# Chebyshev and attention node maps: four blocks of nodes per product, weights on the diagonal, and the product taken term by term

## The chip, the cores and the metric

The kernel runs on one core of one Trainium2 chip. The metric is the time of one execution on the device in microseconds (us). The core has engines that work side by side: TensorE (PE) multiplies and transposes, VectorE (DVE) and ScalarE (ACT) work on elements, GpSimd (POOL) here mostly issues gathers, and SyncE (SP) issues transfers. SP, ACT and POOL each have a queue of their own for transfers, and each engine carries out its instructions in order.

## The reference

A graph network of four layers works on 12500 nodes with 32 features (`x`) and 200000 edges (`src`, `dst`, sorted by `dst`). After each layer the result is added to `x` and normalised. The layer that matters here is the second, two Chebyshev convolutions and one attention. Its `reference` calls come down to this:

```python
def unnL(f):                      # sum of the neighbours' rows
    return segment_sum((f * dinv)[src], dst, n) * dinv
for layer in range(2):            # the same weights W (96 x 32) and b both times
    X0 = feat
    X1 = -re_norm * unnL(X0) + X0 * (re_norm - 1)
    X2 = -2 * re_norm * unnL(X1) + X1 * 2 * (re_norm - 1) - X0
    feat = leaky_relu(concatenate([X0, X1, X2], 1) @ W + b, 0.01)
fs = feat @ Ws + bs               # attention: both maps are 32 x 32
fd = feat @ Wd + bd
e = leaky_relu(fs[src] + fd[dst], 0.2)
# logits e . attn, softmax over the edges of each dst, weighted sum of fs[src]
```

The other three layers are two tensor products over the edges and a plain segment sum.

## The kernel before, in words

The 12500 nodes lie in 98 blocks (`NB`) of 128, one node in each partition, so that a node array is a tile of 128 x 98 x 32. Before the second layer a step of its own scatters the number of edges between pairs of nodes into a matrix of eight-bit counts in memory. A segment sum, `sums` (L657 to L738), then has two halves that run side by side. For the nodes with many edges it multiplies this matrix, loaded piece by piece (L687 alternately on the queues of SP and ACT, L695 on SP), with the rows of the table on PE (L691, L696). For the other nodes POOL gathers the rows of the edges one group of 128 at a time (L715), DVE builds a comparison matrix (L729), and PE and DVE add the rows to their nodes. Before any of this, `sums` loads the indices of the edges (`src`, L669, on SP) and clears the accumulator (L675, DVE).

In front of each sum stands the making of the table. DVE scales X (L788), `split3` (L486 to L489, alternately ACT and DVE) splits it into three 16-bit parts, and `store_table` writes the two halves of the table to memory on the queues of SP (L519) and ACT (L520). The first gather needs the table and the indices.

A Chebyshev layer is: copy X0 (L783, ACT); twice a table and a sum (called c00, c01 in the first layer, c10, c11 in the second) and the elementwise tail (L793 to L798, DVE and ACT); then the dense product with the 96 x 32 weights `wch`. X0, X1 and X2 lie beside each other in one tile `X` with 96 columns for each block. For each block PE transposes 128 x 96 (L805), ACT copies four transposed blocks at once out of PSUM (L807), PE multiplies each with `wch` (L810: the transposed block is the stationary operand, the 32 columns of the weights move), and DVE adds the bias (L811). The leaky rectifier over all nodes (L813) ends the layer.

The attention map has the same form with one source, `h`: transposes of 128 x 32 (L827), copies (L829), products with both 32 x 32 weights, 64 moving columns (L832), and two additions into `fs` and `fd` (L835). Then `fs` is stored as the attention's table and `fd` is split in three (L486 to L489). The attention begins with the load of the edges' indices (L196, SP) and gathers (L207, POOL); it adds the gathered rows at L894.

The order of the instructions on each engine is that in which the program writes them, except that a scheduler lets an instruction pass ahead where its operands allow it; so the clearing of the attention's accumulator (L843, 128 x 9900) stands ahead of the rectifier L813 on DVE. Buffers come from pools whose places overlap when their lives don't; a tile that takes over a place waits for the last use of the tile before it.

Of the kernel before, what the change touches and what calls it, by code (L numbers as in the profile page):

```python
# [11 lines left out]
F32 = mybir.dt.float32  # L12
# [6 lines left out]
ALU = mybir.AluOpType  # L19
AX = mybir.AxisListType  # L20
PSUM = bass.MemoryType.PSUM
# [4 lines left out]
P = 128  # L26
N, E, D, M = 12500, 200000, 32, 8

NB = -(-N // P)
# [31 lines left out]
class Graph:  # L61
# [4 lines left out]
    def __init__(self, ctx, tc, a):  # L66
# [23 lines left out]
        with tc.tile_pool(name="pre", bufs=1) as pre, \  # L90
# [153 lines left out]
class Counts:  # L244
# [12 lines left out]
    def order(self, row16):  # L257
# [5 lines left out]
        with tc.tile_pool(name="row", bufs=1) as rp, \  # L263
# [216 lines left out]
def split3(nc, pool, name, y, shape, y3=None):  # L480

    *outer, n = shape
    if y3 is None:
        y3 = pool.tile([P, *outer, 3, n], BF16, name=f"{name}3")
    r = pool.tile([P, *outer, n], F32, name=f"{name}r")
    nc.scalar.copy(y3[:, :, 0, :], y)  # L486
    nc.vector.tensor_tensor(r, y, y3[:, :, 0, :], op=ALU.subtract)  # L487
    nc.scalar.copy(y3[:, :, 1, :], r)
    nc.vector.tensor_tensor(y3[:, :, 2, :], r, y3[:, :, 1, :], op=ALU.subtract)  # L489
    return y3  # L490
# [22 lines left out]
def store_table(nc, table, x):  # L513

    if len(x.shape) == 4:
        x = x.rearrange("p b k d -> p b (k d)")
    to = table.rearrange("(b p) d -> p b d", p=P)
    h = NB // 2
    nc.sync.dma_start(to[:, :h, :], x[:, :h, :])  # L519
    nc.scalar.dma_start(to[:, h:, :], x[:, h:, :])  # L520
# [3 lines left out]
def kernel(ctx: ExitStack, tc: tile.TileContext, a: dict, out: bass.AP):  # L524
    nc = tc.nc
    gr = Graph(ctx, tc, a)
    ident = gr.ident
# [11 lines left out]
    x = node.tile([P, NB, D], F32, name="x")  # L539
# [213 lines left out]

    with tc.tile_pool(name="l1", bufs=1) as one, ExitStack() as after:
        h = one.tile([P, NB, D], F32, name="h")
        wch = one.tile([3 * D, D], F32, name="wch")
        nc.sync.dma_start(wch, a["cheb_W"])
        wsd = one.tile([D, 2, D], F32, name="wsd")
        nc.sync.dma_start(wsd[:, 0, :], a["gat_W_src"])
        nc.sync.dma_start(wsd[:, 1, :], a["gat_W_dst"])  # L760
        bch = one.tile([P, D], F32, name="bch")
        nc.sync.dma_start(bch, a["cheb_b"][None, :].to_broadcast([P, D]))
        bsd = one.tile([P, 2, D], F32, name="bsd")
# [10 lines left out]
        nc.vector.tensor_scalar(re[:, 1:2], re[:, 4:5], 2.0, -1.0, op0=ALU.mult, op1=ALU.add)  # L774
        nc.vector.tensor_scalar(re[:, 2:4], re[:, 0:2], 2.0, None, op0=ALU.mult)

        with tc.tile_pool(name="cheb", bufs=1) as cp:
            X = cp.tile([P, NB, 3 * D], F32, name="X")
            t = cp.tile([P, NB, D], F32, name="t")
            y3 = cp.tile([P, NB, 3, D], BF16, name="y3")  # L780
            dinv_b = dinv[:, :, None].to_broadcast([P, NB, D])
            for layer in range(2):
                nc.scalar.copy(X[:, :, 0:D], x if layer == 0 else h)  # L783
                for k in range(2):

                    xk = X[:, :, k * D:(k + 1) * D]
                    xn = X[:, :, (k + 1) * D:(k + 2) * D]
                    nc.vector.tensor_tensor(t, xk, dinv_b, op=ALU.mult)  # L788
                    table = tables3[2 * layer + k]
                    with tc.tile_pool(name=f"sp{layer}{k}", bufs=1) as sp:  # L790
                        store_table(nc, table, split3(nc, sp, "y", t, (NB, D), y3))
                    sums(f"c{layer}{k}", table, y3, t)
                    nc.vector.tensor_tensor(t, t, dinv_b, op=ALU.mult)  # L793
                    nc.scalar.activation(xn, xk, AF.Copy, scale=re[:, 2 * k + 1:2 * k + 2])
                    nc.vector.scalar_tensor_tensor(xn, t, re[:, 2 * k:2 * k + 1], xn, op0=ALU.mult,
                                                   op1=ALU.add)
                    if k == 1:
                        nc.vector.tensor_tensor(xn, xn, X[:, :, 0:D], op=ALU.subtract)  # L798
                with tc.tile_pool(name=f"mm{layer}", bufs=3) as work, \
                        tc.tile_pool(name=f"mmps{layer}", bufs=2, space=PSUM) as psum:  # L800
                    for b in range(0, NB, 4):
                        n = min(4, NB - b)
                        pt = psum.tile([3 * D, 4, P], F32, name="pt")
                        for k in range(n):
                            nc.tensor.transpose(pt[:, k, :], X[:, b + k, :], ident)  # L805
                        xt = work.tile([3 * D, 4, P], F32, name="xt")
                        nc.scalar.copy(xt[:, :n, :], pt[:, :n, :])  # L807
                        po = psum.tile([P, 4, D], F32, name="po")
                        for k in range(n):
                            nc.tensor.matmul(po[:, k, :], xt[:, k, :], wch, start=True, stop=True)  # L810
                        nc.vector.tensor_tensor(h[:, b:b + n, :], po[:, :n, :],  # L811
                                                bch[:, None, :].to_broadcast([P, n, D]), op=ALU.add)
                    nc.vector.scalar_tensor_tensor(h, h, 0.01, h, op0=ALU.mult, op1=ALU.max)  # L813
# [5 lines left out]
        with tc.tile_pool(name="gmm", bufs=3) as work, \  # L819
                tc.tile_pool(name="gmmps", bufs=2, space=PSUM) as psum:  # L820
            fs = work.tile([P, NB, D], F32, name="fs", bufs=1)
            fd = work.tile([P, NB, D], F32, name="fd", bufs=1)
            for b in range(0, NB, 4):
                n = min(4, NB - b)
                pt = psum.tile([D, 4, P], F32, name="pt")
                for k in range(n):
                    nc.tensor.transpose(pt[:, k, :], h[:, b + k, :], ident)  # L827
                xt = work.tile([D, 4, P], F32, name="xt")
                nc.scalar.copy(xt[:, :n, :], pt[:, :n, :])  # L829
                po = psum.tile([P, 4, 2, D], F32, name="po")  # L830
                for k in range(n):
                    nc.tensor.matmul(po[:, k, :, :].rearrange("p a d -> p (a d)"), xt[:, k, :],  # L832
                                     wsd.rearrange("p a d -> p (a d)"), start=True, stop=True)
# [14 lines left out]
        with tc.tile_pool(name="selp", bufs=1) as sp:  # L848
            m = sp.tile([3 * C, C], F32, name="m")
# [135 lines left out]
        for k in (1, 2):  # L985
# [7 lines left out]
                                op=ALU.mult)  # L993
# [5 lines left out]
    with tc.tile_pool(name="l2a", bufs=1) as outer:  # L999
        acc3 = outer.tile([P, NBW, 3 * D], F32, name="acc3")  # L1000
        nc.vector.memset(acc3, 0.0)
        with tc.tile_pool(name="l2", bufs=1) as one:
# [35 lines left out]
            with tc.tile_pool(name="nv", bufs=1) as np_:  # L1038
# [13 lines left out]
                                        op=ALU.mult)  # L1052
# [405 lines left out]
```

## Time and profile before

| what | us |
|---|---|
| median of three runs | 12759.83 (12742.87 to 12764.13) |
| profiled execution | 12772.6 |
| its span | 12770.8 |
| busy: POOL, DVE, PE, ACT | 9237.1, 8054.9, 7045.5, 2279.9 |
| first gather of c00, c01, c10 | 4049.00, 4621.68, 5267.02 |
| dense product, first layer | 5164.42 to 5227.35 |
| dense product, second layer | 6383.45 to 6446.24 |
| attention map with what stands ahead of it | 6446.24 to 6530.91 |
| first gather of the attention | 6548.95 |

The times within the span count from its start and come from the instructions in order of time. In a line of the profile, a group of instructions is given by its line in the program, its engine, its operation, what it writes and reads, and the shape; behind the bar stand its busy time and the mean of one in ns, and behind the second bar how long the engine stood idle just before these instructions and what ended that. An engine with q behind its name (SPq, ACTq) is its queue, and PEld is PE's loading of the stationary operand. The granted clock is the share of TensorE's full speed; it is 0.50 or 1.00 at any one moment, and means lie between. Edge work fills most of the span: of the share of each engine above, the second layer's node maps are a small part. An engine's idle time matters only where it lies on the chain that ends last.

### The profile page before, as it was taken

How to read it: one execution, taken by the hardware profiler on the slowest of the kernel's cores; microseconds unless marked ns; L12 is line 12 of the kernel's file. 1: busy time of each engine (PE TensorE's matmuls, PEld its weight loads, DVE VectorE, ACT ScalarE, POOL GpSimd, SP SyncE). 2: the span in 40 equal slices, each digit the busy share in tenths (PEclk: the TensorE clock that was granted, in tenths of full speed). 3: DMA queues.
4: the chain of work that ended last, by engine and by line, in shares of the span. 5: the costliest groups of instructions: out<-in, count | busy, mean ns of one | idle time of the engine just before them, and what ended most of it. 6: DMA issues, size and time to landing. Idle time of an engine off the chain costs nothing.

```text
span 12770.8 us, 151976 instructions
## 1 busy us (share of the span) xinstructions
PE 7045.5 (55%) x44907; PEld 4896.0 (38%) x44908; DVE 8054.9 (63%) x16431; ACT 2279.9 (18%) x4797; POOL 9237.1 (72%) x9125
## 2 busy tenths in 40 slices
PE   3444444000002767676765555553777777777766
PEld 2333333000001444444454444442555555555544
DVE  5655555999001222222247888886999999999932
ACT  0000000000000000000035555552222222222200
POOL 6777774788776767476637777773888888888756
PEclk7677676555556989798856566555555555555588
DMA  4511111332003766566624444442222222222266
GB/s 157 185 16 16 16 17 24 88 86 78 0 0 83 196 183 187 144 189 183 171 66 133 135 133 135 136 137 88 76 73 78 72 77 75 74 75 74 62 176 163
DMA packets 877047, 1296.04 MB, mean 101 GB/s; under 512 B 343752, under 2 KB 561736, under 8 KB 830074
## 3 DMA queue, kind: packets, MB, share of 16 engines
q1 hardware_dynamic: 335420, 720.16, 17.0%
q10 hardware_dynamic: 268900, 436.72, 10.8%
q0 software_dynamic: 271872, 128.86, 8.9%
q8 instruction: 403, 6.60, 0.2%
q14 instruction: 452, 3.70, 0.1%
HBM read 964.92 MB, written 320.08 MB: 101 GB/s over the span
## 4 chain that ended last, share of the span: by engine, by line
DVE 22%; PE 8%; POOL 8%; issue 6%; DMA 2%; ACT 2%; DVEq 2%; ACTq 0%; POOLq 0%; SPq 0%
DVE r L1194 6%; DVE p L1171 4%; POOL g L715 3%; POOL g L207 2%; POOL p L1187 2%; POOL g L1341 2%; PE pf L881 1%; PE pw L1161 1%; DMA g<-table,src 1%; PE ps L964 1%; DVEq L222 1%; PE ps L1233 1%; DVE pr L1122 1%; DVE junk L924 1%; PE po L953 1%
## 5 line engine op out<-in xcount | busy, mean ns | idle before, releaser
L715 POOL DMA_INDIRECT g<-table,src x2080 | 1971.1, 948 | 976.8 <-issue 620.9
L691 PE MATMUL d<-m,y 128*96 128x512 fp8e4 x7350 | 1783.0, 383 | 1280.8 <-DMA m<-matrix 1275.9
L207 POOL DMA_INDIRECT g<-table,src x1568 | 1614.5, 1030 | 665.4 <-issue 444.0
L207 POOL DMA_INDIRECT g<-in_x_dram,src x1568 | 1584.7, 1011 | 476.3 <-issue 438.4
L1341 POOL DMA_INDIRECT g<-table,src x1568 | 1565.6, 998 | 499.3 <-issue 274.9
L691 PEld LDWEIGHTS <-y 128*96 128x96 bf16 x7350 | 939.5, 132 | 1985.7 <-issue 1577.3
L621 PE MATMUL psT<-oh,ft 128*113 128x256 f32 x3136 | 919.9, 465 | 1192.8 <-POOL ft L577 1105.2
L241 DVE TENSOR_TENSOR acc<-acc,ps 128x192 f32 x520 | 183.1, 352 | 2091.7 <-PE ps L238 2002.3
L1194 DVE TENSOR_REDUCE r<-p 128x96 f32<-128x1536 f32 x784 | 1365.3, 1742 | 11.5 <-POOL p L1187 11.5
L415 POOL DMA_INDIRECT matrix<-val,idx x992 | 1122.2, 1131 | 344.6 <-issue 342.4
L1187 POOL TENSOR_TENSOR p<-vs,xk 128x384 f32<-128x384 f32 x1078 | 1082.5, 1005 | 337.3 <-ACT vs L1177 315.0
L1161 PE MATMUL pw<-wz,zT 32*128 32x384 f32 x3136 | 1165.5, 910 | 226.2 <-DVE p L1187 184.4
L621 PEld LDWEIGHTS psT<-oh,ft 128*113 128x113 f32 x3136 | 692.3, 225 | 1420.1 <-POOL ft L577 1148.3
L1171 DVE TENSOR_TENSOR p<-pw,h 128x768 f32<-128x768 f32 x784 | 744.2, 949 | 32.6 <-PE pw L1165 20.7
L624 DVE TENSOR_TENSOR accT<-accT,psT 113x256 f32 x392 | 162.6, 415 | 792.3 <-PE psT L621 788.8
L1165 PEld LDWEIGHTS pw<-wv,hT 32*128 32x128 f32 x3136 | 516.6, 327 | 366.3 <-issue 336.7
L1089 PE MATMUL pd<-xd,kept 128*128 x3136 | 390.0, 252 | 459.7 <-DVE xe L1106 340.1
L1177 ACT COPY vs<-pw 128x256 f32<-128x256 f32 (+1 forms) x588 | 208.3, 354 | 2407.4 <-DVE p L1171 2150.7
L924 DVE CUSTOM_DVE_ANT_0 junk<-pen,pr,mo 128x512 bf16<-128x512 bf16 x784 | 568.6, 744 | 81.5 <-PE pf L881 54.8
L1161 PEld LDWEIGHTS pw<-wz,zT 32*128 32x128 f32 x3136 | 391.9, 303 | 481.3 <-issue 157.8
L471 PE MATMUL ps<-ident,most 128*1 128x128 f32 x1 | 0.4, 372 | 1028.7 <-DVE most L469 1028.7
L881 PE MATMUL pf<-fd,oht 128*128 x3136 | 412.5, 244 | 256.7 <-DVE lr L487 127.2
(314 smaller groups left out, 13988.6 us busy)
## 6 DMA issues: line engine op xcount, KB each, us to landing
m<-matrix ACTq DMA_DIRECT2D x735, 288.0 KB
m<-matrix SPq DMA_DIRECT2D x735, 288.0 KB
kept<-kept SPq DMA_DIRECT2D x196, 1024.0 KB
kept<-oht SPq DMA_DIRECT2D x98, 1024.0 KB
kept<-oh ACTq DMA_DIRECT2D x392, 256.0 KB
matrix<-zero ACTq DMA_DIRECT2D x98, 864.0 KB
g<-table,src POOLq DMA_INDIRECT x5216
row<-keyrow SPq DMA_DIRECT2D x60, 1152.0 KB
```

The costliest lines, as they stand in the source:

```text
L207: nc.gpsimd.indirect_dma_start(out=g[:, c, :], out_offset=None, in_=table[:, :], in_offset=bass.IndirectOffsetOnAxis(ap=src[:, t * C + c:t ...
L415: i = nc.gpsimd.indirect_dma_start(out=to, out_offset=bass.IndirectOffsetOnAxis(ap=idx[:, t:t + 1], axis=0), in_=of[:, t:t + 1], in_offset ...
L621: nc.tensor.matmul(ps, ft[:, q * U + u, :], oh[:, u, :], start=(u == 0), stop=(u == U - 1))
L691: nc.tensor.matmul(banks[k], y3f[:, b, :], m[:, j:j + n], start=(b == 0), stop=(b == NB - 1 and (h, k) != (0, 0)))
L715: nc.gpsimd.indirect_dma_start(out=g[:, c, :], out_offset=None, in_=table[:, :], in_offset=bass.IndirectOffsetOnAxis(ap=src[:, at:at + 1], ...
L881: i = nc.tensor.matmul(ps[:, u, :], oht[:, q, w, u * P:(u + 1) * P], fd3[:, ds(b + w, 1)].rearrange("p o k d -> p (o k d)"), start=(w == 0 ...
L924: nc.vector.tensor_tensor_reduce(junk, pen[:, w, :], pr, 1.0, mo[:, k, :], op0=ALU.add, op1=ALU.max, accum_out=mw[:, k, :])
L1161: nc.tensor.matmul(pw[:, k, 0:384], t.zT[rows, q, :], wzf[rows, :], start=True, stop=True)
L1171: nc.vector.tensor_tensor(t.p[i][:, :, 0:24, :], t.pw[i][:, :, 0:384].rearrange("p k (o c) -> p k o c", c=16), t.h[:, q, v:v + 2, None, 0: ...
L1187: (nc.vector if here else nc.gpsimd).tensor_tensor(t.p[i][:, k, 24:48, :].rearrange("p (k o) i -> p k o i", k=3), of.rearrange("p (o i) -> ...
L1194: nc.vector.tensor_reduce(t.r[:, 2 * i:2 * i + 2, :], t.p[i], AX.X, ALU.add)
L1341: nc.gpsimd.indirect_dma_start(out=g[:, c, :], out_offset=None, in_=tables[1][:, :], in_offset=bass.IndirectOffsetOnAxis(ap=src[:, at:at + ...
```

## The change

The weights are laid out for four blocks at once. `wch` becomes 128 x (3, 4, 32): for each of the three Chebyshev terms a 128 x 128 matrix with the term's 32 x 32 weights four times on the diagonal and zeros elsewhere. `wsd` becomes 128 x (4, 2, 32), 256 columns, in the same way. Both are cleared by DVE and filled by twelve small loads (four on ACT, eight on SP) in place of three.

A new helper `apply` works on up to 16 blocks at a time: up to four transposes, each of four neighbouring blocks (128 x 128), one copy of 128 x 512 on ACT, up to four products with the block-diagonal weights (128 moving columns for a convolution, 256 for the attention map), and one eviction by DVE (two for the map). `convolve(k, ...)` uses it for term k alone. Terms 0 and 1 are multiplied between the storing of their table and the sum, into partial results `hb`; term 2 is multiplied after the second sum and added to `hb`. X becomes three tiles of 128 x 98 x 32. In the order in which each engine gets its instructions, the clearing of the attention's accumulator (L859 after) now stands behind the rectifier (L837 after) and ahead of the map's first additions. In memory on the chip, the index tile of `sums` now lies where the first of the transposed tiles of `convolve` lay, so that its load waits for the last product that reads this one. Outside of these places, each engine's instructions keep their order.

```diff
-        wch = one.tile([3 * D, D], F32, name="wch")
-        nc.sync.dma_start(wch, a["cheb_W"])
-        wsd = one.tile([D, 2, D], F32, name="wsd")
-        nc.sync.dma_start(wsd[:, 0, :], a["gat_W_src"])
-        nc.sync.dma_start(wsd[:, 1, :], a["gat_W_dst"])
+        wch = one.tile([4 * D, 3, 4, D], F32, name="wch")
+        wsd = one.tile([4 * D, 4, 2, D], F32, name="wsd")
+        nc.vector.memset(wch, 0.0)
+        nc.vector.memset(wsd, 0.0)
+        for u in range(4):
+            rows = slice(u * D, (u + 1) * D)
+            nc.scalar.dma_start(wch[rows, :, u, :], a["cheb_W"].rearrange("(k i) o -> i k o", k=3))
+            nc.sync.dma_start(wsd[rows, u, 0, :], a["gat_W_src"])
+            nc.sync.dma_start(wsd[rows, u, 1, :], a["gat_W_dst"])
...
+        def apply(name, y, w, evict):
+            flat = y.rearrange("p b d -> p (b d)")
+            wide = w.shape[1] // 4
+            with tc.tile_pool(name=f"{name}w", bufs=3) as work, \
+                    tc.tile_pool(name=f"{name}p", bufs=2, space=PSUM) as psum:
+                for b in range(0, NB, 16):
+                    n = min(16, NB - b)
+                    parts = [(g, min(4, n - g)) for g in range(0, n, 4)]
+                    pt = psum.tile([P, 4, P], F32, name="pt")
+                    xt = work.tile([P, 4, P], F32, name="xt")
+                    for k, (g, m) in enumerate(parts):
+                        nc.tensor.transpose(pt[:m * D, k, :], flat[:, (b + g) * D:(b + g + m) * D], ident)
+                    k = n // 4
+                    if k:
+                        nc.scalar.copy(xt[:, 0:k], pt[:, 0:k])
+                    if n % 4:
+                        nc.scalar.copy(xt[:n % 4 * D, k], pt[:n % 4 * D, k])
+                    ps = psum.tile([P, 16, wide], F32, name="ps")
+                    for k, (g, m) in enumerate(parts):
+                        nc.tensor.matmul(ps[:, g:g + m, :].rearrange("p b d -> p (b d)"), xt[:m * D, k, :],
+                                         w[:m * D, 0:m * wide], start=True, stop=True)
+                    evict(b, n, ps)
+
+        def convolve(k, xk, to, at):
+            apply(f"mm{k}", xk, wch[:, k].rearrange("p u d -> p (u d)"),
+                  lambda b, n, ps: nc.vector.tensor_tensor(to[:, b:b + n, :], ps[:, :n], at(b, n), op=ALU.add))
...
-            X = cp.tile([P, NB, 3 * D], F32, name="X")
+            X = [cp.tile([P, NB, D], F32, name=f"X{k}") for k in range(3)]
+            hb = cp.tile([P, NB, D], F32, name="hb")
...
                         store_table(nc, table, split3(nc, sp, "y", t, (NB, D), y3))
+                    convolve(k, xk, hb, (lambda b, n: bch[:, None, :].to_broadcast([P, n, D])) if k == 0
+                             else (lambda b, n: hb[:, b:b + n, :]))
                     sums(f"c{layer}{k}", table, y3, t)
...
-                with tc.tile_pool(name=f"mm{layer}", bufs=3) as work, \
-                        tc.tile_pool(name=f"mmps{layer}", bufs=2, space=PSUM) as psum:
-                    for b in range(0, NB, 4):
-                        n = min(4, NB - b)
-                        pt = psum.tile([3 * D, 4, P], F32, name="pt")
-                        for k in range(n):
-                            nc.tensor.transpose(pt[:, k, :], X[:, b + k, :], ident)
-                        xt = work.tile([3 * D, 4, P], F32, name="xt")
-                        nc.scalar.copy(xt[:, :n, :], pt[:, :n, :])
-                        po = psum.tile([P, 4, D], F32, name="po")
-                        for k in range(n):
-                            nc.tensor.matmul(po[:, k, :], xt[:, k, :], wch, start=True, stop=True)
-                        nc.vector.tensor_tensor(h[:, b:b + n, :], po[:, :n, :],
-                                                bch[:, None, :].to_broadcast([P, n, D]), op=ALU.add)
-                    nc.vector.scalar_tensor_tensor(h, h, 0.01, h, op0=ALU.mult, op1=ALU.max)
+                convolve(2, X[2], h, lambda b, n: hb[:, b:b + n, :])
+                nc.vector.scalar_tensor_tensor(h, h, 0.01, h, op0=ALU.mult, op1=ALU.max)
...
-            for b in range(0, NB, 4):
-                n = min(4, NB - b)
-                pt = psum.tile([D, 4, P], F32, name="pt")
-                for k in range(n):
-                    nc.tensor.transpose(pt[:, k, :], h[:, b + k, :], ident)
-                xt = work.tile([D, 4, P], F32, name="xt")
-                nc.scalar.copy(xt[:, :n, :], pt[:, :n, :])
-                po = psum.tile([P, 4, 2, D], F32, name="po")
-                for k in range(n):
-                    nc.tensor.matmul(po[:, k, :, :].rearrange("p a d -> p (a d)"), xt[:, k, :],
-                                     wsd.rearrange("p a d -> p (a d)"), start=True, stop=True)
+            def evict(b, n, ps):
                 for k, o in ((0, fs), (1, fd)):
-                    nc.vector.tensor_tensor(o[:, b:b + n, :], po[:, :n, k, :],
+                    nc.vector.tensor_tensor(o[:, b:b + n, :], ps[:, :n, k * D:(k + 1) * D],
                                             bsd[:, k:k + 1, :].to_broadcast([P, n, D]), op=ALU.add)
+            apply("gm", h, wsd.rearrange("p u k d -> p (u k d)"), evict)
```

More of the change, by code (lines that the diff above doesn't have):

```diff
@@ L782 @@
             for layer in range(2):
-                nc.scalar.copy(X[:, :, 0:D], x if layer == 0 else h)
+                nc.scalar.copy(X[0], x if layer == 0 else h)
                 for k in range(2):
-                    xk = X[:, :, k * D:(k + 1) * D]
-                    xn = X[:, :, (k + 1) * D:(k + 2) * D]
+                    xk, xn = X[k], X[k + 1]
                     nc.vector.tensor_tensor(t, xk, dinv_b, op=ALU.mult)
@@ L797 @@
                     if k == 1:
-                        nc.vector.tensor_tensor(xn, xn, X[:, :, 0:D], op=ALU.subtract)
-                with tc.tile_pool(name=f"mm{layer}", bufs=3) as work, \
-                        tc.tile_pool(name=f"mmps{layer}", bufs=2, space=PSUM) as psum:
-                    for b in range(0, NB, 4):
-                        n = min(4, NB - b)
-                        pt = psum.tile([3 * D, 4, P], F32, name="pt")
-                        for k in range(n):
-                            nc.tensor.transpose(pt[:, k, :], X[:, b + k, :], ident)
-                        xt = work.tile([3 * D, 4, P], F32, name="xt")
-                        nc.scalar.copy(xt[:, :n, :], pt[:, :n, :])
-                        po = psum.tile([P, 4, D], F32, name="po")
-                        for k in range(n):
-                            nc.tensor.matmul(po[:, k, :], xt[:, k, :], wch, start=True, stop=True)
-                        nc.vector.tensor_tensor(h[:, b:b + n, :], po[:, :n, :],
-                                                bch[:, None, :].to_broadcast([P, n, D]), op=ALU.add)
-                    nc.vector.scalar_tensor_tensor(h, h, 0.01, h, op0=ALU.mult, op1=ALU.max)
+                        nc.vector.tensor_tensor(xn, xn, X[0], op=ALU.subtract)
+                convolve(2, X[2], h, lambda b, n: hb[:, b:b + n, :])
+                nc.vector.scalar_tensor_tensor(h, h, 0.01, h, op0=ALU.mult, op1=ALU.max)
         att = after.enter_context(tc.tile_pool(name="att", bufs=1))
@@ L818 @@
         nc.vector.memset(fd3[:, NB:, :, :], 0.0)
[L819 to L822, printed above, removed]
-            for b in range(0, NB, 4):
-                n = min(4, NB - b)
-                pt = psum.tile([D, 4, P], F32, name="pt")
-                for k in range(n):
-                    nc.tensor.transpose(pt[:, k, :], h[:, b + k, :], ident)
-                xt = work.tile([D, 4, P], F32, name="xt")
-                nc.scalar.copy(xt[:, :n, :], pt[:, :n, :])
-                po = psum.tile([P, 4, 2, D], F32, name="po")
-                for k in range(n):
-                    nc.tensor.matmul(po[:, k, :, :].rearrange("p a d -> p (a d)"), xt[:, k, :],
-                                     wsd.rearrange("p a d -> p (a d)"), start=True, stop=True)
+        with tc.tile_pool(name="gmm", bufs=1) as work:
+            fs = work.tile([P, NB, D], F32, name="fs")
+            fd = work.tile([P, NB, D], F32, name="fd")
+            def evict(b, n, ps):
                 for k, o in ((0, fs), (1, fd)):
-                    nc.vector.tensor_tensor(o[:, b:b + n, :], po[:, :n, k, :],
+                    nc.vector.tensor_tensor(o[:, b:b + n, :], ps[:, :n, k * D:(k + 1) * D],
                                             bsd[:, k:k + 1, :].to_broadcast([P, n, D]), op=ALU.add)
+            apply("gm", h, wsd.rearrange("p u k d -> p (u k d)"), evict)
             store_table(nc, tables[0], fs)
```

## The prediction, on record before the changed kernel ran

> **What bounds the kernel now.** I read the page first, then the groups by line and shape in the two stretches that the change rewrites, then the busy time by stretch, then the order of time at the start of a segment sum. From the page (the first line is the granted TensorE clock in tenths, in 40 slices):
>
> ```profile
> PEclk7677676555556989798856566555555555555588
> ...
> L715 POOL DMA_INDIRECT g<-table,src x2080 | 1971.1, 948 | 976.8 <-issue 620.9
> ```
>
> Each segment sum issues 416 gathers; 0.948 us and 0.30 of issue each make 520 us, which is what a sum takes. So a sum ends a fixed time after its first gather, and whatever delays that gather delays the kernel. Between two sums the work is a chain. Its piece in layer 0 is the dense product, from the end of L798 (5164.42) to the end of the last L811 (5227.35), 62.9 us; layer 1 has the same, 6383.45 to 6446.24. Groups by shape in it:
>
> ```profile
> L810 PE MATMUL po<-wch,xt 96*128 96x32 f32 x196 | 44.9, 394 | 0.0
> ...
> L805 PE MATMUL pt<-ident,X 128*96 128x128 f32 x98 | 26.1, 423 | 17.4 <-DVE X L798 17.4
> ...
> L811 DVE TENSOR_TENSOR h<-po,bch 128x128 f32<-128x128 f32 x24 | 7.0, 292 | 55.1 <-PE po L810 55.1
> ```
>
> DVE waits for PE (55.1), and so does ACT (67.5 idle before L807); PE's 98 transposes and 196 passes (a float32 product is two) follow one another every 213 ns. Then the attention map, 6446.24 to 6530.91:
>
> ```profile
> L832 PE MATMUL po<-wsd,xt 32*128 32x64 f32 x196 | 48.0, 423 | 0.5 <-ACT xt L829 0.5
> ...
> L827 PE MATMUL pt<-ident,h 128*32 128x128 f32 x98 | 25.2, 415 | 14.0 <-DVE h L813 14.0
> ...
> L843 DVE MEMSET acc<- 128x9900 f32 x1 | 8.3, 8308 | 2.0 <-issue 2.0
> ```
>
> The clearing of the accumulator, L843, runs ahead of L813 while PE stands (14.0 idle). Busy time by stretch (PE, PEld, DVE, ACT, POOL, then the clock):
>
> ```profile
> 5190.00:5227.00 37.00, 37.00 (x175) 34.50 (x175) 4.38 (x15) 8.50 (x15) 0.00 (x0) 0.50 0.00 1
> ...
> 6460.00:6531.00 71.00, 70.02 (x294) 55.56 (x294) 12.19 (x50) 14.14 (x25) 0.00 (x0) 0.50 0.07 12
> ```
>
> PE is full and alone, at half clock. The start of a sum in order of time:
>
> ```profile
> 5246.33 3.42 DVE L489 TENSOR_TENSOR y<-yr,y 128x3136 bf16<-128x3136 f32 x1 [2.92 <-ACT y L488]
> ...
> 5249.78 0.38 SPq L519 DMA_DIRECT2D table<-y  x1
> ...
> 5250.55 9.56 SPq L669 DMA_DIRECT2D src<-in_src_col_dram  x1
> ...
> 5266.83 2.13 PE L691 MATMUL d<-m,y 128*96 128x512 fp8e4 x5 [39.75 <-DMA m<-matrix]
> 5267.02 0.94 POOL L715 DMA_INDIRECT g<-table,src  x1 [125.09 <-DMA m<-matrix]
> ```
>
> Call the end of L489 E (5249.75). The index load L669 sits in SP's queue behind the table until E+10.4, the table lands near E+14.7, and the first gather starts at E+17.3. In that gap PE has nothing to do.
>
> **The change part by part.** The profiled execution took 12772.6 us (span 12770.8), 12.8 above the median of 12759.8; the sum is made against it and 12.8 is taken off at the end.
>
> *The product left at a layer's end.* Of three Chebyshev terms only the last is still multiplied after the sums. PE's instructions: 98/4 = 25 transposes and 25 products of two passes, 75 in place of 294. A pass with 128 moving columns is priced by L1150 and L805, both 128 wide and 213 ns apart at clock 0.50: 75 x 0.213 = 16.0 us, and 1.2 for first wait and last add (L811's last is 0.23). At half clock that is 17.2.
>
> *The clock.* The kernel has the other state. L691 at 4048.90 takes 2.08 us for five 512-wide products; at 4053.09, after the clock went from 0.50 to 1.00 (4053.05), 1.14. L621, 256 wide, is spaced 427 ns at 0.50 and 216 at 1.00. I counted what share of the 3.41 us (the grid of the clock's records) ahead of each rise was filled by PE at its spacing: 0.79 at least, mostly 0.92 or more, in rises with L621, 0.74 at least with L691, while L1142 at up to 0.78 stayed at 0.50. So a share above 0.8 raised it. L810 fills its time too and stayed cold, but it moves 32 columns in the 213 ns in which L805 moves 128: counted by columns layer 0's stretch is half full. The new stretch has 128 columns in every pass and no gap, so I let it rise 3.4 to 6.8 us after it starts, 5.1 taken. Then 5.1 + (16.0 - 5.1)/2 + 0.6 = 11.2 us. Gain: 62.9 - 11.2 = 51.7, twice: 103. (At half clock 45.7 each.)
>
> The Trainium skill, "TensorE: Matmul & The Clock Gate", Part 4, says of transpose mode that the full clock "doesn't engage" for it, since it does not count as busy in the same way. By that the new stretch would be 50/75 = 0.67 busy and stay at half clock, which is the second case below. This trace speaks against it in part: in the 3.41 us before the rise at 6647.2, L953 (16-bit transposes) held 0.50 and L964 0.31. No run here shows a float32 transpose on either side.
>
> *The attention map.* 25 transposes and 25 products with 256 moving columns. A 256-wide pass is L621's 427 ns: 25 x 0.213 + 50 x 0.427 = 26.7 at half clock. Ahead of it stand L837 (leaky, 3.4 as L813) and 0.15. DVE then clears fd3, mx and the accumulator (9.2 with L843's 8.31) before its first add, so with two PSUM buffers PE stops after two products until 10.7; the five remaining transposes fit there. Then 3.5 + 10.7 + four products of 1.71 + 0.4 + last adds 1.0 = 22.4 us with the clock up, 29.5 at half clock. Now 84.7 us; gain 62, or 55. The clearing, now on the path, is covered by PE's first two products; without them it would cost 8.3 again.
>
> *Start of attention.* The index load L196 was issued at 6543.9, when fd's split (L489) was done, and its gather began at 6548.95; now it waits for no split, but for the fs table, whose second half landed at 6537.3. The table's first half, which was issued at 6498.2 under PE, now leaves late too and shares the rings. The first addition of gathered rows, L894, started at 6570.40 after 8.65 of waiting for them. Bounds: 0 and 6.4 (6543.9 - 6537.5). I take 4.5.
>
> *The two early products.* These run between table and sum. The first two groups of transposes need only X and run ahead of E; from E+1.15 (copies on ACT, behind its table store) 67 passes are left, 14.3 us at half clock. With the rise after 5.1: E + 1.15 + 5.1 + 4.6, near E+11. The index load's buffer overlies the transposed tile of this product, so L669, every SP load behind it, and POOL's first gather wait for that. E+11 is when the load left the ring anyway (E+10.4): 0 to 1 each, 0.5 taken, 2 for the four sums. What hides these products is the table's way to memory; a faster store would put all of their time on the path. At half clock the product ends at E+16; the load then takes the 5.0 that lies between 6543.93 and 6548.95, and the gather is at E+21.1, 3.9 later, 15.6 for the four. ACT's two loads of m now stand behind seven copies of 0.58; DVE's clearing of acc (3.82) behind seven adds of 0.69: both end before the first gather's rows.
>
> *Weights and X.* X in three tiles changes no count of elements: L788, L795 and L798 stay at 3.4 each, the copy L783 at 2.8; I cost that at nothing. Twelve small loads in place of three, two memsets; lam, which landed at 4019.79, comes behind them on SP and L487 ran at 4021.85. Bounds 0 and 3; 1.5 taken.
>
> Sum: -103 -62 -4.5 +2 +1.5 = -166, so 12606.6 for an execution like the profiled one, 12593.8 against the median.
>
> **Rivals.** *PE stays at half clock.* For: the transposes, if they don't count; the pauses in the map. Against: the shares above. -91.4 -55 -4.5 +15.6 +1.5 = -133.8, 12626.
>
> *The early products hold the sums back further.* For: all SP loads and POOL stand behind one tile, and after it the index load meets the table's tail. Each gather 10 us late instead of 0.5 to 3.9: four times 10, on half clock: 12650.
>
> *Slower: a pass of 128 columns with 128 rows of weights costs double.* Place: PE in all seven products. With the product's time c, the early product ends at E+c-1.2 and the gather starts 5.1 later; the gains are 2(62.9-c), 84.7-4.1-1.67c and 4.5, the costs 4(c-13.4) and 1.5. They meet at c = 34 us, a pass of 0.44 us. At 0.64 us (c = 49) the sum is +113: 12873. Against: L1134, 128x128 with 128 columns, is 213 ns apart; 0.427 is what 256 columns take.
>
> *The work was hidden.* For: DVE and ACT are hardly busy there. Against: POOL idle 125.09 up to the gather at 5267.02, across the whole product. It would give 12760.
>
> **How the numbers follow.** Clock up 0.55 (12594, own range 12580 to 12610), half clock 0.28 (12626), sums held back 0.09 (12650), hidden 0.02, slower 0.03, and 0.03 for more gain than summed. The forecast is the first, 12594. The range goes up to half clock with some of the third case, 12645, and down to 12572: the early rise (3.4 us) in all products and 6.4 at attention's start take off 8, and the runs before spread 17 below their median. The bound of what can be told from no change is 0.2%, 25 us: faster 0.95, same 0.02, slower 0.03.
>
> **What would show it.** In the profile after: each last convolution near 11 us at a clock above 0.5 (17 at 0.50 for the second case); the map near 22; the first gather at E+17 to E+18 (E+21 in the second case); 416 gathers still 520 us; L894's wait under 5. Wrong if a pass of 128 columns is spaced more than 0.25 us, or if the first gather moves by more than 4.

## The result, and the profile after

The changed kernel takes 12601.93 us (median of four runs, 12597.98 to 12603.82) against 12751.35 for the kernel before in the same comparison (12741.52 to 12764.13): a ratio of 0.9882 with a 95% interval of 0.9865 to 0.9899, 149.4 us less. The forecast was faster, 12594, with a range of 12572 to 12645.

The profiled execution of the changed kernel has a span of 12599.2 us, 171.6 less than the one before. Not all of that is the change: the last scatter of the edge counts, which no edit touches, ended at 3987.95 in place of 4010.84. These 22.9 us are a difference between two executions of the same work, and they fit the profiled execution of before, which was 21 above that kernel's median (the changed kernel itself has 4017.43 in another profile, e7). So stretches are compared below, each against its own start:

| stretch, us | before | after | difference | forecast |
|---|---|---|---|---|
| last scatter to the end of the first table's split | 20.73 | 20.73 | 0 | +1.5 |
| end of the split (E) to the last gather, four sums together | 2148.4 | 2162.4 | +14.0 | +2 |
| dense product, layer 0 | 62.93 | 13.22 | -49.7 | -51.7 |
| dense product, layer 1 | 62.93 | 13.46 | -49.5 | -51.7 |
| from there to the last addition of the attention map | 84.67 | 23.96 | -60.7 | -62 |
| from there to the first addition of gathered rows | 39.48 | 38.86 | -0.6 | -4.5 |
| sum | | | -146.5 | -166 |

With 22.9 and 146.5, 2.2 of the 171.6 are left for the stretches that are the same in both kernels.

The groups by shape in layer 0's dense product, from 5149.0 to 5162.4 of the profile after (the columns are those of before):

```profile
L802 PE MATMUL ps<-wch,xt 128*128 128x128 f32 x48 | 7.8, 329 | 0.5 <-ACT xt L797 0.5
...
L809 DVE TENSOR_TENSOR h<-ps,hb 128x512 f32<-128x512 f32 x6 | 4.2, 692 | 8.6 <-PE ps L802 8.6
L794 PE MATMUL pt<-ident,X 128*128 128x128 f32 x24 | 4.0, 323 | 17.5 <-DVE X L835 17.5
...
L797 ACT COPY xt<-pt 128x512 f32<-128x512 f32 x6 | 3.3, 586 | 28.3 <-PE pt L794 28.3
```

72 instructions of full width and three narrow ones stand where 294 stood. The clock in the two halves of this product and of the map (start and end, length, busy time of PE, PEld, DVE, ACT and POOL, granted clock):

```profile
5149.00:5154.40 5.40, 5.20 (x24) 4.96 (x25) 0.75 (x2) 1.17 (x2) 0.00 (x0) 0.50 0.01 3
5154.50:5162.00 7.50, 6.57 (x53) 5.70 (x51) 3.46 (x5) 2.41 (x5) 0.00 (x0) 1.00 0.00 0
6343.20:6349.00 5.80, 5.78 (x17) 4.76 (x18) 3.79 (x2) 1.17 (x2) 0.00 (x0) 0.50 0.01 3
6349.20:6363.50 14.30, 11.46 (x59) 9.06 (x57) 12.09 (x15) 2.51 (x5) 0.00 (x0) 1.00 0.21 33
```

The clock rises 5.2 us after the first transpose of the product (5149.20 to 5154.44) and 5.9 after the map's. Before, 0.50 stood through all of it.

The start of a sum, c01, in order of time (E is 4585.40):

```profile
4581.98 3.42 DVE L489 TENSOR_TENSOR y<-yr,y 128x3136 bf16<-128x3136 f32 x1 [2.87 <-ACT y L488]
...
4586.56 3.78 PE L802 MATMUL ps<-wch,xt 128*128 128x128 f32 x16 [15.46 <-ACT xt L797]
...
4598.13 0.23 DVE L809 TENSOR_TENSOR hb<-ps,hb 128x64 f32<-128x64 f32 x1 [0.25 <-PE ps L802]
4598.17 0.33 SPq L669 DMA_DIRECT2D src<-in_src_col_dram  x1
...
4601.20 3.82 DVE L675 MEMSET acc<- 128x4512 f32 x1 [0.89 <-DVE rel L671]
...
4604.36 2.88 POOL L715 DMA_INDIRECT g<-table,src  x1 [53.90 <-DMA me<-early]
...
4604.95 2.32 DVE L729 TENSOR_SCALAR oh<-iotab,rel 128x256 bf16<-128x256 bf16 x12
...
4607.55 0.94 POOL L715 DMA_INDIRECT g<-table,src  x1 [0.30 <-issue]
```

The early product ends at E+12.7, the index load L669 leaves right behind it, and the first gather starts at E+19.0, 1.9 later than before. What is new is its length: 2.88 us in place of 0.94. It lies across the clearing of acc (L675) and the first comparisons (L729) on DVE, and ends when these end. It is so in three of the four sums; in c00 it ends 0.9 behind the clearing, while the comparisons are still running. In the four sums the first gather takes 5.22, 2.88, 3.73 and 3.18 us, and the second one starts at E+22.3, 22.2, 22.5 and 22.2, where it was E+18.3 to E+18.7 before. All gathers behind it keep the old spacing of 1.25.

### The profile page after: what moved, and what is told of

Its sections match the earlier page's. It is cut to its first block, busy times and chain, and to the rows that moved or that the text cites. A ratio compares the mean times of both kernels' runs of the same rounds, so it can differ in the third digit from the quotient of the medians.

```text
span 12599.2 us, 151149 instructions
## 1 busy us (share of the span) xinstructions
PE 6948.9 (55%) x44550; PEld 4802.4 (38%) x44551; DVE 8062.8 (64%) x16389; ACT 2259.6 (18%) x4771; POOL 9231.4 (73%) x9125
## 3 DMA queue, kind: packets, MB, share of 16 engines
q1 hardware_dynamic: 335596, 720.17, 17.2%
## 4 chain that ended last, share of the span: by engine, by line
POOL 28%; DVE 26%; issue 12%; PE 9%; DMA 4%; ACT 2%; DVEq 2%; SPq 0%; ACTq 0%; POOLq 0%
POOL g L715 13%; DVE r L1210 6%; POOL matrix L415 6%; POOL g L207 4%; DVE p L1187 4%; DMA g<-table,src 2%; DVE eq L438 2%; POOL p L1203 2%; POOL g L1357 2%; POOL early L415 1%; PE pw L1177 1%; DVE n L399 1%; PE pf L897 1%; PE ps L1249 1%; DVE pr L1138 1%
## 5 line engine op out<-in xcount | busy, mean ns | idle before, releaser
L1210 DVE TENSOR_REDUCE r<-p 128x96 f32<-128x1536 f32 x784 | 1364.9, 1741 | 11.7 <-POOL p L1203 11.7
L1187 DVE TENSOR_TENSOR p<-pw,h 128x768 f32<-128x768 f32 x784 | 743.7, 949 | 32.3 <-PE pw L1181 20.5
```

The lines of the kernel that those rows point to most:

```text
L1187: nc.vector.tensor_tensor(t.p[i][:, :, 0:24, :], t.pw[i][:, :, 0:384].rearrange("p k (o c) -> p k o c", c=16), t.h[:, q, v:v + 2, None, 0: ...
L1210: nc.vector.tensor_reduce(t.r[:, 2 * i:2 * i + 2, :], t.p[i], AX.X, ALU.add)
```

## The experiments

The four runs e1 to e4 come from a chip on which transfers took longer, gathers above all (the kernel before took 15529.53 us there), so of them only stretches without paced gathers are used, not totals. On the chip of e5 to e8 the kernel before took 12768.49.

Theory W said that the sums begin late because the index load waits for the early product; theory C, that DVE's preparation of the sum, pushed behind the product's additions, meets the first gather. The edits are shown in part; "..." marks what is left out.

**e1: the index tile loaded once, in a place of its own.**

```diff
-                src = one.tile([P, (NTICK - ST) * C], I32, name="src")
-                nc.sync.dma_start(src, a["src_col"][:, ST * C:])
+                src = once.get("src")
...
+            once["src"] = cp.tile([P, (NTICK - ST) * C], I32, name="srcs")
+            nc.sync.dma_start(once["src"], a["src_col"][:, ST * C:])
             for layer in range(2):
```

> Against the changed kernel: the index tile of the sums is loaded once, ahead of the first sum, into a place of its own, so that no first gather waits for a load behind the early product. In the changed kernel the time from the end of the table's split (E) to the last gather is 540.2 to 541.1 us in the four sums, before it was 536.4 to 537.7; 14.0 us in all. Theory W (the wait of the index load makes all of it): the first gather starts near E+16 and the stretch comes back to 536 to 537. Theory C (the sum's own preparation on DVE, the clearing of acc above all, now falls on the first gather, which took 2.9 to 5.2 us in place of 0.94): the first gather starts near E+16, but it or the next ones are stretched until DVE's clearing ends near E+21, and the stretch stays at 539 to 541.

The second gather of the four sums started at E+18.1, 22.2, 22.5 and 21.6, against E+22.3, 22.2, 22.5 and 22.2 with the wait. Three of four moved by 0.5 or less, though no load stands ahead of them. (The stretch to the last gather can't be read on this chip.) c01 of this run in order of time, E at 5100.25:

```profile
5116.05 3.82 DVE L679 MEMSET acc<- 128x4512 f32 x1 [0.89 <-DMA me<-early]
5118.36 3.74 POOL L719 DMA_INDIRECT g<-table,srcs  x1 [105.90 <-DMA m<-matrix]
5119.79 2.32 DVE L733 TENSOR_SCALAR oh<-iotab,rel 128x256 bf16<-128x256 bf16 x12
```

The gather starts at E+18.1 and is stretched to E+21.9, the end of the comparisons. In c00 one gather slipped through ahead of the clearing, but the second then lasted from 4311.85 to 4316.30, across the clearing from 4311.57 to 4315.39. So W alone falls.

**e2: acc in a place of its own, cleared by POOL while it waits for the table.**

```diff
-                acc = one.tile([P, NBW - BF, 3 * D], F32, name="acc")
-                nc.vector.memset(acc, 0.0)
+                acc = once.get("acc")
...
+            once["acc"] = cp.tile([P, NBW - BF, 3 * D], F32, name="accs")
             for layer in range(2):
...
+                    nc.gpsimd.memset(once["acc"], 0.0)
                     nc.vector.tensor_tensor(t, xk, dinv_b, op=ALU.mult)
```

> Against the changed kernel: acc has a place of its own and POOL clears it while it waits for the table; DVE clears nothing ahead of the sum, and the index load still waits for the early product. Theory W: the first gather starts at E+18.7 and takes 3 to 5 us as now; the stretch from E to the last gather stays near 540.5. Theory C: it starts at E+18.7 and takes 0.95; the stretch comes to 538 to 538.5, 2 to 3 us less in each sum, 8 to 11 in all.

c01 in order of time, E at 5092.00:

```profile
5104.62 0.33 SPq L671 DMA_DIRECT2D src<-in_src_col_dram  x1
...
5106.80 2.44 DVE L733 TENSOR_SCALAR oh<-iotab,rel 128x256 bf16<-128x256 bf16 x12
...
5110.31 0.95 POOL L719 DMA_INDIRECT g<-table,src  x1 [42.02 <-DMA src<-in_src_col_dram]
5111.56 0.94 POOL L719 DMA_INDIRECT g<-table,src  x1 [0.30 <-issue]
```

The load leaves at E+12.6 as before, the comparisons are over at E+17.2, and the first gather takes 0.95 to 0.98 in all four sums. The second one starts at E+18.0, 19.6, 19.9 and 19.7: 2.4 to 4.4 earlier, 12.0 us in all, where theory C had expected 8 to 11. Against e4, whose sums are those of the changed kernel on this same chip (second gathers at E+22.5, 22.2, 21.3 and 22.2), it is 11.0. So theory C is shown: with DVE's clearing gone, the first gather is issued at its old length. The comparisons alone hold it hardly at all. In c00 of this run they lie across the first two gathers, with no clearing near:

```profile
4312.51 2.60 DVE L733 TENSOR_SCALAR oh<-iotab,rel 128x256 bf16<-128x256 bf16 x12
4312.74 0.98 POOL L719 DMA_INDIRECT g<-table,src  x1 [31.53 <-DVE rel L673]
4314.03 1.02 POOL L719 DMA_INDIRECT g<-table,src  x1 [0.30 <-issue]
```

Why a gather that had met the clearing mostly ended with the comparisons, and not before them, stays open.

The Trainium skill, "SBUF — State Buffer", section "SBUF: two separate sides", describes such a stall: POOL writes the descriptors of its transfers through ports that it shares with DVE, and waits while an operation of DVE holds them. The runs agree on the stall. The page names filling as such an operation for another chip alone; here a fill did it (e1's second gather, 4.45 us with only the fill beside it for the first 3.5).

**e3: all three products at the layer's end.**

```diff
-                    convolve(k, xk, hb, (lambda b, n: bch[:, None, :].to_broadcast([P, n, D])) if k == 0
-                             else (lambda b, n: hb[:, b:b + n, :]))
                     sums(f"c{layer}{k}", table, y3, t)
...
+                convolve(0, X[0], hb, lambda b, n: bch[:, None, :].to_broadcast([P, n, D]))
+                convolve(1, X[1], hb, lambda b, n: hb[:, b:b + n, :])
                 convolve(2, X[2], h, lambda b, n: hb[:, b:b + n, :])
```

> Against the changed kernel: the products of the first two terms stand behind the second sum, beside that of the third, with the same block-diagonal weights. If the early place hides them but for what the sums show: the four sums go back to 537 each (-14 in all) and each layer's end grows by two products at the full clock, 8 to 9.5 us each (+32 to +38 for both layers); total +18 to +24. Rival (the early place gains nothing, since a product at full clock fits under the elementwise tail): total -14 to 0. Rival (the clock falls between the products): 13 us each, total +38.

The dense products at the layers' ends took 28.76 and 29.29 us: 15.7 and 16.0 more, 32 us for both, against a mean of 13.0 and 13.3 in the other three runs of this chip. The elementwise tail ahead of them took 11.35 in place of 10.41 in each layer, because additions of the late product stand among its steps on DVE: 1.9 more for both. The second gathers were back at E+18.3 to 18.9 (first ones 0.94 to 0.97), 13.7 earlier than in e4, which is the 14 that the sums lost. So the early place is worth about 32 + 2 - 14 = 20 us, within the first expectation. Its price of 8 to 9.5 us for a further product at full clock is not what stood behind it, though. In two stretches of layer 0's end, and in the last product alone:

```profile
5875.00:5885.10 10.10, 7.97 (x34) 7.29 (x35) 3.89 (x6) 1.17 (x2) 0.00 (x0) 0.50 0.00 0
5885.20:5905.00 19.80, 16.99 (x136) 14.99 (x134) 8.79 (x15) 5.89 (x12) 0.00 (x0) 1.00 0.00 1
5893.90:5905.00 11.10, 9.53 (x75) 8.42 (x75) 4.42 (x8) 3.48 (x7) 0.00 (x0) 1.00 0.00 0
```

A whole product at full clock took 11.0 us, and the clock was at 0.50 for the first 9 of the stretch; against that, part of the first product ran under the tail. The 15.7 is the sum of these, not the price of two products.

**e4: the old attention map behind the new convolutions.** The edit puts the old loop (L827 to L835 of the kernel before) back, with its 32 x 64 weights.

> Against the changed kernel: the attention map is the old one (98 blocks one by one, 64 moving columns), the convolutions are the new ones. If the map's gain is its own: from the end of the last convolution to the last addition of the map 84.7 us again if the accumulator is cleared ahead of the leaky rectifier, 74 if it is cleared behind it (23.96 in the changed kernel); total +50 to +61. If the new order of the gathers' start was worth what I said: 3 to 5 us more. Rival (the map's gain came from the convolution's clock, which is still up): the old map runs at the full clock, 35 to 45 us.

The map took 69.40 us from the rectifier's end, 72.9 from the last convolution, near the 74 expected for a clearing behind the rectifier; with the new map it is 20.5 to 22.2 in the other runs of this chip. The rival, the old map at the full clock in 35 to 45 us, is out: the clock was up for one piece of 3.41 us alone, the third of these stretches.

```profile
7533.30:7536.68 3.38, 3.38 (x16) 3.28 (x16) 3.29 (x1) 0.48 (x1) 0.00 (x0) 0.50 0.00 0
7536.70:7540.10 3.40, 3.40 (x17) 1.89 (x16) 3.40 (x1) 1.71 (x3) 0.00 (x0) 0.50 0.01 2
7540.12:7543.50 3.38, 2.06 (x19) 1.72 (x17) 2.58 (x7) 0.22 (x1) 0.00 (x0) 1.00 0.00 0
```

This place tells what the clock went by. PE is full in the first two stretches, with 16 instructions of 213 ns each, and the stationary operand is a quarter of a full 128*128 in both (32*128 and 128*32). In the first they are products with 64 moving columns, and the clock stayed down behind them; in the second they are transposes with 128, while PE ran ahead during the clearing, and the clock rose behind them at 7540.1. So how long PE was busy and how much of the array was filled do not decide it. That the second are transposes doesn't either: products with 128 columns raised the clock in the changed kernel. What is left is the moving columns. On DVE, in order of time:

```profile
7527.73 3.42 DVE L836 SCALAR_TENSOR_TENSOR h<-h 128x3136 f32<-128x3136 f32 x1
7531.13 0.14 DVE L841 MEMSET fd<- 128x96 uint32 x1
```

The rectifier follows the convolution's last addition at once, and the clearing (L866, 8.31 us) begins at 7533.39. So the 10.2 us that stood ahead of the rectifier before (L843 and its wait) left with the convolutions' new form, which changed the order on DVE, and not with the map's product. In this run the attention's first gather took 0.94 us and began 18.26 behind the map, the second 19.51; with the new map they begin at 14.40 (and the first takes 3.95) and at 18.65. The new start is worth under 1 us, not the 3 to 5 expected.

**e5: 120 idle transposes ahead of each early product.**

```diff
+                    with tc.tile_pool(name=f"wm{layer}{k}", bufs=1, space=PSUM) as wm:
+                        pw = wm.tile([P, 4, P], F32, name="pw")
+                        for j in range(120):
+                            nc.tensor.transpose(pw[:, j % 4, :], xk[:, 0:4, :].rearrange("p b d -> p (b d)"), ident)
                     convolve(k, xk, hb, (lambda b, n: bch[:, None, :].to_broadcast([P, n, D])) if k == 0
```

> Against the changed kernel: PE carries out 120 more float32 transposes (of one group of four blocks, into a PSUM tile that nothing reads) ahead of each early product, in the time in which it waits for the table's split. If transposes count for the clock: it rises 3.4 to 6.8 us after they start and is up when the product starts, the first group takes 1.8 us for 16 passes in place of 3.6, the product ends at E+9.5 to E+11.5 (E+12.7 in the changed kernel), and the first gather starts 1 to 2 us earlier. If they don't count: the clock stays at 0.50 through 25.6 us of transposes, the product starts near E+10 to E+13 and ends near E+25, and each first gather comes 8 to 14 us later, total +35 to +55.

Three stretches ahead of and in the sum c00: two of the idle transposes alone, and the product:

```profile
4012.30:4015.50 3.20, 3.20 (x15) 3.20 (x16) 3.20 (x1) 0.00 (x0) 0.00 (x0) 0.50 0.15 22
4015.60:4026.90 11.30, 11.30 (x105) 11.30 (x104) 6.01 (x7) 8.44 (x3) 0.00 (x0) 1.00 0.03 4
4028.00:4038.60 10.60, 8.54 (x71) 7.56 (x68) 4.42 (x7) 3.48 (x7) 0.00 (x0) 1.00 0.89 159
```

With nothing but float32 transposes on PE, the clock rose after 3.3 us (2.9 to 5.5 in the other sums) and stayed up: 15 of them took 3.20 us, then 105 took 11.30. They count. The sentence of the Trainium skill ("TensorE: Matmul & The Clock Gate", Part 4) that the prediction set against its own count doesn't hold here. The product ran at full clock from its start, E+1.2 to E+10.5, and the second gathers came at E+20.0 to 20.7, 1.5 to 2.5 earlier: the whole preparation on DVE moves with the product's end. The total of this one run, 12622.52, lies within the spread of e7 and shows nothing of it.

**e6: the attention's accumulator cleared by POOL.**

```diff
-        nc.vector.memset(acc3, 0.0)
+        nc.gpsimd.memset(acc3, 0.0)
```

> Against the changed kernel: POOL, which is idle then, clears the attention's accumulator in place of DVE (8.31 us). If DVE's clearing holds the map back: the first addition starts when PE's first product of 16 blocks is done, near 5.5 us behind the rectifier in place of 10.4, and from the rectifier's end to the last addition it takes 15.5 to 17.5 us in place of 20.5. If it is covered by PE's first two products, as I said: 19.5 to 20.5.

From the rectifier's end to the last addition 18.47 us, against 20.50 and 22.18 in two executions of the changed kernel; the first addition came 5.53 behind the rectifier in place of 10.46. DVE's clearing does hold the map back, by 2.0 to 3.7 us, less than expected. The attention's first two gathers still took 1.78 and 3.04 us, with this clearing gone from DVE; here they lie beside its smaller steps (L866 to L868, L182). The total, 12627.22 in this one run, shows nothing of the gain: the tail of the second layer's last sum took 28.2 us there and 22.7 in e7, a difference that this one run leaves open.

**e7 and e8: the changed kernel again, and one with e1, e2 and e6 together.**

> The changed kernel as it is, for comparison on the same chip with the one below: about 149 us under the kernel before (12602 against 12751).

> The changed kernel with the index tile loaded once, acc in a place of its own and cleared by POOL ahead of the table, and the attention's accumulator cleared by POOL. If both theories hold (the wait and the collision): first gather near E+16 and 0.95 long, the stretch from E to the last gather 535.5 to 537, and the map 3 to 5 us shorter; 18 to 25 us under the changed kernel, 12577 to 12584. If only the wait costs: 8 to 10 less. If neither: the same within 3.

e7 is 12625.16 us (12617.14 to 12630.31), 143 under the kernel before where 149 had been expected, ratio 0.9885 with an interval of 0.9869 to 0.9902. e8 is 12604.26 (12595.33 to 12610.68), 0.987 with 0.9853 to 0.9886: 20.9 us under e7 by the medians, as expected (18 to 25), and 164 under the kernel before. The two ratios' intervals overlap, but the ranges of the runs don't, and the stretches say where it comes from: the four sums 2149.1 in place of 2162.1 (-13.1; the kernel before had 2148.4), the map 18.47 in place of 22.18 (-3.7), the first addition of gathered rows 37.5 behind the map in place of 39.4 (-1.9). Its profile has another 7 us less in the attention behind that, which no edit explains and one profile doesn't settle. c01 in order of time, E at 4613.34:

```profile
4628.28 2.44 DVE L735 TENSOR_SCALAR oh<-iotab,rel 128x256 bf16<-128x256 bf16 x12
...
4631.11 0.95 POOL L721 DMA_INDIRECT g<-table,srcs  x1 [41.61 <-DVE oh L735]
...
4632.37 0.94 POOL L721 DMA_INDIRECT g<-table,srcs  x1 [0.31 <-issue]
```

The comparisons end at 4630.72, just ahead of the first gather. The first gathers start at E+16.5 to 17.9, later than the E+16 expected, and the stretches to the last one are 536.4 to 537.9 (535.5 to 537 expected). Still, the early products now cost the sums less than 1 us in all: the table's way to memory covers them, as the prediction had it, once DVE is out of POOL's way.

e7 also shows why the map took 22.18 there and 20.50 in the first profile. Four stretches of its map:

```profile
6370.00:6375.60 5.60, 5.60 (x17) 4.62 (x18) 3.59 (x2) 1.17 (x2) 0.00 (x0) 0.50 0.01 3
6375.70:6382.40 6.70, 4.85 (x29) 3.78 (x29) 6.70 (x5) 1.66 (x3) 0.00 (x0) 1.00 0.00 0
6382.50:6385.90 3.40, 3.40 (x9) 2.67 (x9) 1.51 (x3) 0.58 (x1) 0.00 (x0) 0.50 0.00 0
6386.00:6390.60 4.60, 4.60 (x23) 3.74 (x21) 2.70 (x5) 0.26 (x1) 0.00 (x0) 1.00 0.38 60
```

In the second, PE is busy for 4.85 of 6.70 us, since it waits for the first additions, which wait for the clearing. The clock then falls for one piece of 3.41 us, in which the products take twice as long. In the last 3.41 us ahead of the fall PE was busy for 1.80 (6379.08 to 6382.49); the same place of the first profile has 1.90 (6352.53 to 6355.93), and there the clock stayed up.

## Why the prediction was right, and where it was off

The forecast (clock up, faster by 166) came true in direction and in its main terms; 146.5 were measured in the stretches and 149.4 by the medians. The forecast time, 12594, lies 8 under the measured one. That is closer than the terms deserve: the median of before came out at 12751.35 with its fourth run, 8.5 lower than the one used.

- *What bounds the kernel.* Right: gathers stayed at 1.25 us each, and whatever moved the first ones moved the end of the sum. e3 and e8 show it in both directions.
- *The clock.* Right: it rose 5.2 us into the product where 5.1 was taken. The count of columns, not of time, fits the old stretch, which stayed at half clock; e4 shows it within one run, and e5 that transposes belong in the count. The second case (half clock, 12626) is out.
- *The product left at a layer's end.* Mis-sized: 13.2 to 13.5 in place of 11.2. I let PE run without a gap behind the rise. It does so at half clock; at full clock two groups take 3.2 us (5154.52 to 5157.69) where 24 x 0.107 = 2.57 was assumed, since eight transposes are followed by a stop for ACT's copies (5155.29, the last transpose's start, to 5155.80), and the last group of two blocks pays transpose, copy, product and addition one behind the other, 1.4 us.
- *The attention map.* 23.96 in place of 22.4. The sum let PE stand until DVE's clearings and first additions were over, 10.7 behind the rectifier; it was 11.7 (6354.81). The clearings were taken as 9.2 and ended at 10.5: the 2.0 us of wait ahead of L843, which its row shows, were left out. The rest is 8.8 in place of 8.2. The sentence that the clearing is "covered by PE's first two products" failed too: PE's two products were done near 7.7. e6 puts its price at 2.0 to 3.7, part of it through the clock (e7). That the clearing left the place ahead of the rectifier was right, 10.2 us; e4 shows that this belongs to the convolutions' edit.
- *The two early products.* The step that failed most: +14.0 in place of +2. The start of the first gather was nearly right (0.6 earlier to 1.9 later, 0 to 1 forecast), though the product ended at E+12.7 and not near E+11, with the same stops at full clock as above. Wrong was the sentence that DVE's clearing would end ahead of the first gather's rows, and so be harmless: I asked when DVE's work is needed, and not what it does to POOL while it runs. The first gather, which before had stood free, 8 us behind DVE's last comparison, was stretched by 2 to 4 us in each sum, and e1 and e2 show that the clearing does it.
- *Start of attention.* 0.6 in place of 4.5. The gather did begin 14.4 us behind the map in place of 18.0, but took 3.95, beside DVE's preparation of the attention, so that the second one began 18.7 behind it (19.3 before). The first addition waited 7.99 for the rows (8.65 before), where under 5 was forecast. This looks like the same stall as in the sums; no run took these steps off DVE, and so it isn't shown.
- *Weights and X.* Nothing in place of 1.5: the twelve loads were covered.
- *The rivals.* Sums held back further: the place was right (+14 against +40), the cause another one. Half clock, double passes and hidden work are out by the clock and the table above.

## What to carry to other kernels

Small matrices can be put on the diagonal of a full one: 75 instructions for a map in place of 294, full width for PE, and with it the full clock, which products with 32 and 64 moving columns did not bring here, though PE was busy throughout. (A convolution now needs three such products, 225 instructions, two of them in gaps.) When a product moves into a gap, list what else used that gap and where it goes then: here DVE's preparation slid from a free place onto POOL's first gather and gave back 14 of the 34 us that the early place saved. A clearing that may run anywhere belongs on an engine that is idle, ahead of the critical start, and in a place of its own so that it doesn't have to wait.

## What the runs showed of the hardware that was not expected

A fill of 128 x 4512 float32 on DVE (3.82 us) held the issue of a gather on POOL, so that it took 2.9 to 5.2 us in place of 0.94, while twelve comparisons in 16 bits hardly did (0.98 and 1.02 in e2); POOL's own fill of 128 x 9900 took 8.35 us, as long as DVE's 8.31. Float32 transposes alone raised the clock from 0.50 to 1.00 within 2.9 to 5.5 us. Behind 3.4 us of transposes with 128 moving columns the clock rose, and behind 3.4 us of products with 64, just as full, it did not (e4). In two executions of the same map, 1.80 us of work in a piece of 3.41 us lost the full clock for the next piece, and 1.90 kept it (e7 and the first profile). And two executions of the same unchanged first third of the kernel differed by 22.9 us, more than most single terms of this study, so that only stretches, not totals, could tell them.
